# Experts' outputs scattered to their tokens' places by indirect writes, the last block combined by products

## The chip, the cores and the metric

The kernel runs on one core of a Trainium2 chip. Its engines work side by side, each on its own stream of instructions in order: PE (TensorE, matrix products and transposes; PEld is its weight load), DVE (VectorE), ACT (ScalarE), POOL (GpSimd) and SP (SyncE, which here only issues DMAs). SP's and ACT's DMAs go through hardware queues; POOL's, the indirect ones among them, through a software queue whose descriptors POOL builds itself. The metric is the device time of one execution in microseconds (us), the median over runs.

## What is computed

The reference is an attention layer, then a conditioned low-rank layer feeding a transformer block whose feed-forward part is a mixture of experts. Only the last part is touched by the change:

```python
logits = x @ router_weight                       # 8192 tokens, 8 experts
probs = jax.nn.softmax(logits, axis=-1)
top_p, top_i = jax.lax.top_k(probs, 2)
top_p = top_p / jnp.sum(top_p, axis=-1, keepdims=True)
...
cap = int(np.ceil(N * K / E * 1.25))             # an expert's later tokens are dropped
...
fc1 = gelu(einsum('ech,ehf->ecf', xt, moe_w1))   # 256 -> 512
fc2 = einsum('ecf,efh->ech', fc1, moe_w2)        # 512 -> 256
weighted = fc2 * padded_probs[:, None]
moe_out = zeros((N, H)).at[padded_tid].add(weighted)
return h1 + moe_out                              # and the block's input is added
```

So each of 8192 tokens (256 numbers each) gets the sum of at most two expert outputs, weighted by two probabilities, on top of a residual.

## The kernel before

**Stages.** Stage 1 (loop over `s`, 32 sequences of 256 tokens, to about 360 us) computes the attention layer and the low-rank layer. Its instructions are ordered by a planner; SP loads the input of sequence `s + 3` while `s` is computed. The second stage (loop over `i`, 64 tiles of 128 tokens, to about 690 us) computes the transformer block's attention, writes each token's normalised row to `z2_d` and its residual to `res_d` in HBM. From here on the order on every engine is the order in which the program is written. The third stage runs the experts: the tokens are sorted into *slots*, 256 slots make a *block*, and all tokens of a block go to one expert. Three plans exist, for 54, 62 or 74 blocks; the number is computed on the device and a branch takes one. Here 54 blocks run.

**Routing.** `packed`, `early` and `rest` compute, in small pieces laid between blocks, for each token its two slots (`slots`), and by products with one-hot matrices (`p_tab`, L1572) the inverse: for each slot the token's number (`rows_of` writes it to `src_row`). The first 11 blocks come from the first 48 tiles alone (`early`), so that they can start before the last tiles are done. The token's number travels as the upper 16 bits of a float: `rowbits` holds `IDBASE + token`, and `rows_of` shifts it back and subtracts `IDBASE`. `yrow` holds, for each token, its two slots, and `prob` its two weights, set to zero where the token was dropped.

**One block n.** `gather(n)` (L763) is two indirect DMAs on POOL, each fetching 128 rows of 1 KB from `z2_d`; it is issued three blocks ahead and waits for one of four buffers. `turn_in` (L783, L787) transposes the rows on PE and scales them on DVE. `weights` (L775) copies the expert's weights. `hidden` (L797, L801) makes 16 products and the gelu on ACT; `result` (L809) makes 16 products, ACT copies them to `ys` (L813, two buffers), and SP writes the block's 256 rows to `y_d` in slot order (L814).

**Bringing rows back.** 16 groups of four tiles. From block 20 the loop is in `experts`. Group g is fetched when block `ready[g]` has come: at 22, 24, 26 and so on, and the last one after all 54. `fetch_rows` (L1694) issues for each tile two indirect DMAs on POOL that fetch its tokens' expert rows from `y_d[:upto]`, where `upto` is the number of slots that are then written; SP reads the group's residual `rs` (L1688). `combine` (L1705) is two DVE operations a tile: row times weight plus residual. Four DMAs on SP (L1711) write a group's output. In one block's time POOL is given two gathers and four of these fetches. Order on POOL in loop pass n: `gather(n + 3)`, then the fetches of up to two tiles.

**Waits.** The program declares no semaphores: the framework orders an instruction behind earlier ones that touch the same part of a buffer, in SBUF, PSUM or HBM. The views that are passed to indirect DMAs are cut by hand in two places: early gathers name `z2_d[: 3 * PACK * P]`, and the fetches name `y_d[:upto]`.

Of the kernel before, what the change touches and what calls it, by code (L numbers as in the profile page):

```python
# [9 lines left out]
F32 = mybir.dt.float32  # L10
I32 = mybir.dt.int32
BF16 = mybir.dt.bfloat16
AF = mybir.ActivationFunctionType
ALU = mybir.AluOpType
AX = mybir.AxisListType
PSUM = bass.MemoryType.PSUM
DRAM = bass.MemoryType.DRAM

P = 128
S = 32  # L20
T = 256
D = 256
# [3 lines left out]
NTOK = S * T  # L26
NJ = NTOK // P
# [12 lines left out]
EARLY = 3  # L40
IDBASE = 96 * 128
DR = D + NE
# [7 lines left out]
def block_kernel(ctx: ExitStack, tc: tile.TileContext, a: dict, out: bass.AP):  # L50
# [20 lines left out]
    res_d = dram.tile([NSG, P, 4 * D], F32, name="res_d")  # L71
    y_d = dram.tile([NB * BLK, D], F32, name="y_d")
    fac_d = dram.tile([S, RANK, 2 * D + NE], F32, name="fac_d")
# [36 lines left out]
    with ExitStack() as c1:  # L110
# [456 lines left out]
        for b in range(4):  # L567
# [37 lines left out]
        nc.vector.memset(freshc[:, :, 0], 0.0)  # L605
        rowbits = const.tile([P, NJ], I32, name="rowbits")
        nc.gpsimd.iota(rowbits, pattern=[[P, NJ]], base=IDBASE, channel_multiplier=1)
        nc.vector.tensor_scalar(rowbits, rowbits, 16, None, ALU.logical_shift_left)
        rb2 = const.tile([P, NJ, 2], BF16, name="rb2")
        nc.vector.tensor_copy(  # L610
            rb2, rowbits.bitcast(F32).unsqueeze(2).to_broadcast([P, NJ, 2])
        )
# [14 lines left out]
        prow_s = const.tile([P, 1], F32, name="prow_s")  # L627
        nc.vector.tensor_scalar(prow_s, prow, float(BLK), None, ALU.mult)

        wqkv = load(const, "wqkv", [P, 2, 384], a["wqkv"].rearrange("(c p) m -> p c m", p=P))  # L630
# [15 lines left out]

        rb2c = const.tile([P, PACK, 2], BF16, name="rb2c")
        for q in range(3):
            for b in range(4):
                r = SURE * (4 * q + b)  # L650
                nc.sync.dma_start(
                    out=rb2c[r : r + SURE],
                    in_=rb2[32 * b : 32 * b + SURE, PACK * q : PACK * (q + 1)],
                )
# [21 lines left out]
        head.close()  # L676

        for s in range(2, S + 1):  # L680
            if s + 3 < S:
                load_x(s + 3)
            if s < S:
                softmax(s)
# [51 lines left out]
    gap = keep.tile([P, NJ], F32, name="gap")  # L736
    yrow = keep.tile([P, NJ, 2], I32, name="yrow")
    src_row = keep.tile([P, NB, 2], I32, name="src_row")
    eids = [keep.tile([1, P], I32, name=f"eid{i}") for i in range(2)]
    plan = keep.tile([P, 1], I32, name="plan")  # L740
# [3 lines left out]
    bothc = keep.tile([P, 2 + NE * PACK], BF16, name="bothc")  # L744
    slots1 = keep.tile([P, NJ, 2], F32, name="slots1")
    in1 = keep.tile([P, NE, 3 * PACK], BF16, name="in1")
    other = keep.tile([P, NE, 3 * PACK], BF16, name="other")
    nc.gpsimd.memset(slots1, 0.0)
    nc.gpsimd.memset(in1, 0.0)
# [55 lines left out]
    def result(n, ps):  # L805
        we2 = wcs[n % 2][:, 1].rearrange("p (c d) -> p c d", c=4)
        for h in range(2):
            for f in range(4):
                nc.tensor.matmul(  # L809
                    ps[:, h, :], lhsT=hts[n % 2][:, f, h * P : (h + 1) * P],  # L810
                    rhs=we2[:, f, :], start=(f == 0), stop=(f == 3),
                )
        nc.scalar.copy(yss[n % 2], ps)  # L813
        nc.sync.dma_start(  # L814
            out=y_d[BLK * n : BLK * (n + 1), :].rearrange("(p h) d -> p h d", h=2),
            in_=yss[n % 2],
        )

# [18 lines left out]
    with ExitStack() as c2:  # L837
# [276 lines left out]
        def early():  # L1114
# [95 lines left out]
            for q in range(3):  # L1210
                for b in range(4):
                    r, rows = SURE * (4 * q + b), slice(32 * b, 32 * b + SURE)
                    js = slice(PACK * q, PACK * (q + 1))
                    nc.sync.dma_start(
                        out=slots1[rows, js, :].rearrange("p j k -> p (j k)"),
                        in_=slots[r : r + SURE],
                    )
                    nc.sync.dma_start(
                        out=in1[rows, :, js], in_=by_expert(inc)[r : r + SURE]
                    )  # L1220
# [24 lines left out]
            for i in range(n2):  # L1245
# [3 lines left out]
                )  # L1249
            rows_of(ps[:, :nbc], cut(nbc, I32), src_row[:, :EARLYB, :])  # L1250
            begun.append(True)
# [38 lines left out]

        def rows_of(table, tab, rows):


            nc.vector.tensor_scalar(tab, table.bitcast(I32), 16, None, ALU.logical_shift_right)
            nc.vector.tensor_scalar(
                rows.rearrange("p n h -> p (n h)"), tab, IDBASE, 0, ALU.subtract, ALU.max
            )
# [90 lines left out]
    with tc.tile_pool(name="rt", bufs=1) as rt, tc.tile_pool(  # L1388
# [24 lines left out]
        def rest():  # L1413
# [165 lines left out]
            for g in range(0, n2 // 8 + 2, 2):  # L1579
# [3 lines left out]
                for k in range(g, min(g + 2, n2 // 8)):  # L1583
# [8 lines left out]
                    columns(rows, col[:, 16 * k : 16 * k + 16], nbc)  # L1592
                    numbered(rows, rb2[:, 4 * k : 4 * k + 4])
                    ready.append((oh, wid, k))
                    yield 1.8
            rows_of(p_tab, rt.tile([P, nbc], I32, name="tab"), src_row[:, EARLYB:, :])
            begun.append(True)
# [23 lines left out]
            for k in range(2):  # L1621
                nc.vector.tensor_scalar(
                    prob[:, :, k], half, 0.5 - k, 0.5, ALU.mult, ALU.add
                )

            all_ = slots1.rearrange("p j k -> p (j k)")
            moved = rt.tile([P, n2], F32, name="moved")
            nc.vector.tensor_scalar(
                moved, slots, 0.0, float(EARLYB * BLK), ALU.is_gt, ALU.mult
            )  # L1630
            nc.vector.tensor_tensor(moved, moved, slots, ALU.add)
            nc.vector.tensor_tensor(moved, moved, all_, ALU.add)
            yield 1.0
            probf = prob.rearrange("p j k -> p (j k)")
            nc.vector.scalar_tensor_tensor(probf, moved, 0.0, probf, ALU.is_gt, ALU.mult)
            nc.vector.tensor_scalar(
                yrow.rearrange("p j k -> p (j k)"), moved, -1.0, 0.0, ALU.add, ALU.max
            )
            yield 0.4

# [36 lines left out]

    def experts(count, ready, w3):

        groups = [{} for _ in range(NSG)]  # L1680

        def fetch_rows(j):

            g, i = j // 4, j % 4
            v = groups[g]
            if i == 0:
                v["rs"] = w3.tile([P, 4, D], F32, name="rs")
                nc.sync.dma_start(  # L1688
                    out=v["rs"].rearrange("p j d -> p (j d)"), in_=res_d[g]
                )  # L1690
            upto = ready[g] * BLK
            for k in range(2):
                yg = v[i, k] = w3.tile([P, D], F32, name=f"yg{k}", bufs=8)
                nc.gpsimd.indirect_dma_start(  # L1694
                    out=yg, out_offset=None, in_=y_d[:upto, :],
                    in_offset=bass.IndirectOffsetOnAxis(ap=yrow[:, j, k : k + 1], axis=0),
                )

        def combine(j):
            g, i = j // 4, j % 4  # L1700
            v = groups[g]
            if i == 0:
                v["ot"] = w3.tile([P, 4, D], F32, name="ot")
            for k in range(2):
                nc.vector.scalar_tensor_tensor(  # L1705
                    v["ot"][:, i, :], v[i, k], prob[:, j, k : k + 1],
                    v["rs"][:, i, :] if k == 0 else v["ot"][:, i, :], ALU.mult, ALU.add,
                )
            if i == 3:
                for b in range(4):  # L1710
                    nc.sync.dma_start(  # L1711
                        out=out_v[b, :, 4 * g : 4 * g + 4, :],
                        in_=v["ot"][32 * b : 32 * b + 32],
                    )


        fetched, due = 0, []
        for n in range(AHEAD, count):
            if n + 3 < count:
                gather(n + 3)  # L1720
            for f2 in range(2):
                hidden(n, f2, p_hs[f2])
            if n + 1 < count:
                turn_in(n + 1, p_x)
                weights(n + 1)
            result(n, p_ys[n % 2])
            while due and due[0][0] <= n:
                combine(due.pop(0)[1])
            for _ in range(2):
                if fetched < NJ and ready[fetched // 4] <= n:  # L1730
                    fetch_rows(fetched)
                    due.append((n + 2, fetched))
                    fetched += 1
        while due or fetched < NJ:
            while fetched < NJ and len(due) < 8:
                fetch_rows(fetched)
                due.append((0, fetched))
                fetched += 1
            combine(due.pop(0)[1])

    def arm(count, ready):
        with tc.tile_pool(name="w3", bufs=2) as w3, tc.manual_schedule():
            experts(count, ready, w3)

# [62 lines left out]
```

## Time and profile before

| | us |
|---|---|
| median of 15 runs | 1136.94 (1133.82 to 1143.35) |
| the profiled execution | 1138.14 |
| its span | 1136.4 |
| PE busy in it | 1056.5 (93%) |
| POOL busy | 509.5 (45%) |
| DVE busy | 680.0 (60%) |
| ACT busy | 411.9 (36%) |

A profile is one execution, recorded by the hardware. Its span runs from the first to the last recorded work; 1.7 us lie around it. In tables of groups, `L763` is line 763 of the kernel; a line reads *line, engine, operation, output <- inputs, number of instructions | busy us, mean ns of one | idle us of the engine just before them, and what ended most of it*. In the chain of waits and the timeline the first number is the start in us from the span's beginning, the second the length. The slices cut the span into 40 equal parts of 28.4 us; a digit is the busy share in tenths. "To landing" is the time from a DMA's issue until what waits for it can go on.

### The profile page before, as it was taken

What the parts mean: (1) busy time and instruction counts of PE and PEld (TensorE: products, weight loads), DVE (VectorE), ACT (ScalarE), POOL (GpSimd) and SP (SyncE); (2) the same over time, 40 slices, a digit from 0 to 9 for tenths busy, and PEclk for the clock granted to TensorE, in tenths of its full rate; (3) what the DMA queues carried; (4) which work ended last, traced back from release to release, by engine and by line L of the source; (5) the groups of instructions that cost most, each with busy time, mean ns of one, the idle gap of its engine ahead of it and who ended that gap; (6) DMA issues with size and microseconds to landing.
All of it is one profiled execution on the core that took longest, in us unless ns stands there. A gap on an engine that the chain in (4) does not pass through costs nothing.

```text
span 1136.4 us, 16889 instructions
## 1 busy us (share of the span) xinstructions
PE 1056.5 (93%) x5723; PEld 855.4 (75%) x5724; DVE 680.0 (60%) x1676; ACT 411.9 (36%) x953; POOL 509.5 (45%) x687
## 2 busy tenths in 40 slices
PE   8999999999994999999999778999999998999992
PEld 5686888888883777777776566888888887887871
DVE  4454555555552688888888886972222554454542
ACT  2222333333332556666665343432222222222220
POOL 2011111111111466666665465213333777777774
PEclk9999999999997999999999998999999999999996
DMA  9552333333262132534343143112223566555665
GB/s 304 140 149 95 102 112 112 112 112 113 84 161 88 58 128 99 188 132 170 126 140 114 39 136 134 65 48 79 72 72 107 181 193 208 179 184 184 198 180 161
DMA packets 88147, 149.50 MB, mean 132 GB/s; under 512 B 13620, under 2 KB 54100, under 8 KB 87508
## 3 DMA queue, kind: packets, MB, share of 16 engines
q1 hardware_dynamic: 72068, 99.97, 27.3%
q0 software_dynamic: 15936, 48.32, 13.9%
q8 instruction: 47, 0.77, 0.3%
q14 instruction: 48, 0.39, 0.1%
q10 hardware_dynamic: 48, 0.05, 0.0%
HBM read 90.86 MB, written 57.22 MB: 130 GB/s over the span
## 4 chain that ended last, share of the span: by engine, by line
PE 51%; issue 24%; DMA 8%; POOL 8%; DVE 7%; SPq 1%; ACT 1%; POOLq 0%; ACTq 0%; DVEq 0%
PE ps_y L809 11%; PE ps_h L797 10%; PE p_qkv L885 6%; DMA yg<-y_d,yrow 4%; PE p_pr L990 4%; PE p_av L956 4%; PE p_sc L915 3%; PE ps_t L944 3%; DMA xx<-z_d,src_row 3%; POOL xx_d L507 2%; POOL o L503 2%; POOL yg L1694 2%; PE ps_xt L783 2%; PE ps_n L846 1%; PE ps_f L271 1%
## 5 line engine op out<-in xcount | busy, mean ns | idle before, releaser
L809 PE MATMUL ps_y<-xx,ht 128*128 128x256 f32 x864 | 201.5, 387 | 0.0
L797 PE MATMUL ps_h<-xt,xx 128*128 128x256 f32 x864 | 195.8, 379 | 0.0
L809 PEld LDWEIGHTS ps_y<-xx,ht 128*128 128x128 f32 x864 | 164.1, 195 | 21.6 <-ACT ht L801 0.3
L797 PEld LDWEIGHTS ps_h<-xt,xx 128*128 128x128 f32 x864 | 163.6, 190 | 22.1
L763 POOL DMA_INDIRECT xx<-z_d,src_row x108 | 122.3, 1133 | 128.3 <-PE ps_xt L783 76.9
L787 DVE TENSOR_SCALAR xt<-ps_xt,ln 128x256 f32<-128x256 f32 x106 | 52.7, 539 | 194.8 <-PE ps_xt L783 194.8
L1694 POOL DMA_INDIRECT yg<-y_d,yrow x128 | 135.2, 1056 | 55.8 <-issue 28.8
L502 POOL TENSOR_SCALAR ve<-mv 128x2 f32<-128x2 f32 x32 | 6.9, 217 | 255.1 <-DVE mv L103 255.1
L801 ACT ACTIVATE ht<-ps_h 128x512 f32<-128x512 f32 x108 | 64.5, 597 | 127.4 <-PE ps_h L797 127.2
L813 ACT COPY ys<-ps_y 128x512 f32<-128x512 f32 x54 | 31.6, 586 | 189.3 <-PE ps_y L809 174.7
L885 PE MATMUL p_qkv<-wqkv,lnt 128*128 128x384 f32 x256 | 94.4, 492 | 0.0
L935 POOL TENSOR_TENSOR sc<-sc,mx 128x512 f32<-128x512 f32 x64 | 66.9, 1046 | 52.1 <-DVE mx L934 47.9
L895 ACT COPY vbd<-p_qkv 32x64 f32<-32x64 f32 x256 | 52.5, 205 | 94.9 <-DVE qk L891 92.7
L956 PEld LDWEIGHTS p_av<-vbd,pt 128*128 128x128 f32 x512 | 67.0, 192 | 18.9 <-ACT pt L949 3.7
L990 PE MATMUL p_pr<-wp,ao 128*128 128x264 f32 x256 | 71.8, 403 | 3.1 <-DVE h L994 3.0
L995 POOL TENSOR_TENSOR res<-h,xx 128x256 f32<-128x256 f32 x64 | 43.7, 683 | 62.3 <-DVE h L994 60.2
L378 PE MATMUL p_z<-yt,m_qk 128*128 128x256 f32 x256 | 67.2, 389 | 0.8 <-ACT yt L363 0.8
L495 PE MATMUL p<-layer,x1t 128*128 128x264 f32 x256 | 65.9, 401 | 2.1 <-ACT x1t L485 1.5
L956 PE MATMUL p_av<-vbd,pt 128*128 128x68 f32 x512 | 65.1, 270 | 1.5 <-ACT pt L949 1.5
L391 PE MATMUL p_v<-w_vo,yt 128*128 128x256 f32 x256 | 60.6, 379 | 0.0
L495 PEld LDWEIGHTS p<-layer,x1t 128*128 128x128 f32 x256 | 46.8, 193 | 15.6 <-ACT x1t L485 7.4
L885 PEld LDWEIGHTS p_qkv<-wqkv,lnt 128*128 128x128 f32 x256 | 44.4, 193 | 18.3 <-ACT lnt L849 1.1
(312 smaller groups left out, 1844.1 us busy)
## 6 DMA issues: line engine op xcount, KB each, us to landing
xx_d<-o POOLq DMA_DIRECT2D x32, 530.0 KB, 3.4
y_d<-ys SPq DMA_DIRECT2D x54, 256.0 KB
xx<-xx_d SPq DMA_DIRECT2D x13, 1060.0 KB
xt<-in_x_t_dram SPq DMA_DIRECT2D x32, 256.0 KB
xs<-in_x_dram SPq DMA_DIRECT2D x32, 256.0 KB
wall<-in_moe_w_dram SPq DMA_DIRECT2D x16, 512.0 KB
z_d<-h SPq DMA_DIRECT2D x16, 512.0 KB
res_d<-res SPq DMA_DIRECT2D x16, 512.0 KB
```

The costliest lines, as they stand in the source:

```text
L378: nc.tensor.matmul(p_z[:, m, :], lhsT=m_qk[:, c, m * P : (m + 1) * P], rhs=yt[:, c, :], start=(c == 0), stop=(c == 1),)
L391: nc.tensor.matmul(p_v[:, t, :], lhsT=yt[:, c, t * P : (t + 1) * P], rhs=w_vo[:, c, :], start=(c == 0), stop=(c == 1),)
L495: nc.tensor.matmul(p_2, lhsT=v["x1t"][:, c, t * P : (t + 1) * P], rhs=v["layer"][:, c, :], start=(c == 0), stop=(c == 1),)
L763: nc.gpsimd.indirect_dma_start(out=xgs[n % 4][:, h, :], out_offset=None, in_=z2_d[: 3 * PACK * P, :] if n < EARLYB else z2_d[:, :], in_off ...
L797: nc.tensor.matmul(ps[:, i, :], lhsT=we1[:, c, f * P : (f + 1) * P], rhs=xts[n % 2][:, c, :], start=(c == 0), stop=(c == 1),)
L801: nc.scalar.activation(hts[n % 2][:, 2 * f2 : 2 * f2 + 2, :], ps, AF.Gelu_apprx_tanh)
L809: nc.tensor.matmul(ps[:, h, :], lhsT=hts[n % 2][:, f, h * P : (h + 1) * P], rhs=we2[:, f, :], start=(f == 0), stop=(f == 3),)
L885: nc.tensor.matmul(ps, lhsT=live2[n // 4]["lnt"][:, c, j * P : (j + 1) * P], rhs=wqkv[:, c, :], start=(c == 0), stop=(c == 1),)
L935: nc.gpsimd.tensor_tensor(sc, sc, mx.unsqueeze(2).to_broadcast([P, 16, S]), ALU.subtract)
L956: nc.tensor.matmul(p_a[:, g // 2, :, g % 2, :], lhsT=v["pt"][:, g, :], rhs=vbd[n % 5][:, g], start=True, stop=True,)
L990: nc.tensor.matmul(p_p, lhsT=tiles[n]["ao"][:, gp, :], rhs=wp2[:, gp, :], start=(gp == 0), stop=(gp == 1),)
L1694: nc.gpsimd.indirect_dma_start(out=yg, out_offset=None, in_=y_d[:upto, :], in_offset=bass.IndirectOffsetOnAxis(ap=yrow[:, j, k : k + 1], a ...
```

## The change

The expert's rows no longer go to `y_d` in slot order, to be fetched by token; they are written straight to the token's place and read back in plain transfers.

- `y_d` becomes 2 x 8192 rows, one for each token and each of its two choices, and 128 dump rows for empty slots. `rowbits` counts tokens once for each choice, `IDBASE` becomes 8192, and `rows_of` makes two tables: `src_row` (the token) and `dst_row` (the place in `y_d`, or the partition's dump row where the slot is empty).
- `result` issues two indirect writes on POOL, 128 rows of 1 KB each, instead of one plain write on SP.
- Stage 1 fills `y_d` with zeros, in 64 plain writes of 256 KB on SP, three in each pass from `s = 4`, so that rows of dropped tokens read as zero; `yrow` and the zeroing of `prob` go.
- `fetch_rows` reads a group's rows in four plain DMAs of 256 KB on SP, ahead of `hidden(n)` in the order. The loop's order on POOL becomes `gather(n + 3)`, then the scatters of block n.
- In the plans of 54 and 62 blocks the last block is not written to `y_d`. The last group is read one block earlier; what the last block adds to its 512 tokens is computed by products on PE with a matrix `own` that holds each token's weight at its slot. `own` is prepared in blocks 20 to 24: per tile three DVE operations, two transposes and one copy.

```diff
-    y_d = dram.tile([NB * BLK, D], F32, name="y_d")
+    y_d = dram.tile([2 * NTOK + P, D], F32, name="y_d")
...
+            for n in range(3 * s - 12, min(3 * s - 9, NTOK // P)) if s > 3 else ():
+                nc.sync.dma_start(
+                    out=y_d[2 * P * n : 2 * P * (n + 1), :].rearrange("(p r) d -> p (r d)", r=2),
+                    in_=zeros,
+                )
...
         nc.scalar.copy(yss[n % 2], ps)
-        nc.sync.dma_start(
-            out=y_d[BLK * n : BLK * (n + 1), :].rearrange("(p h) d -> p h d", h=2),
-            in_=yss[n % 2],
-        )
+        for h in range(2):
+            nc.gpsimd.indirect_dma_start(
+                out=y_d[:, :], in_=yss[n % 2][:, h, :], in_offset=None,
+                out_offset=bass.IndirectOffsetOnAxis(ap=dst_row[:, n, h : h + 1], axis=0),
+            )
...
-        def rows_of(table, tab, rows):
+        def rows_of(table, tab, more, ns):
             nc.vector.tensor_scalar(tab, table.bitcast(I32), 16, None, ALU.logical_shift_right)
             nc.vector.tensor_scalar(
-                rows.rearrange("p n h -> p (n h)"), tab, IDBASE, 0, ALU.subtract, ALU.max
+                src_row[:, ns, :].rearrange("p n h -> p (n h)"), tab, NTOK - 1, 0,
+                ALU.bitwise_and, ALU.bitwise_or,
+            )
+            nc.vector.tensor_scalar(more, tab, 0.0, dump[:, 0:1], ALU.is_equal, ALU.mult)
+            nc.vector.scalar_tensor_tensor(
+                dst_row[:, ns, :].rearrange("p n h -> p (n h)"), tab, -float(IDBASE), more,
+                ALU.add, ALU.add,
             )
...
+        def mark(i):
+            ms = []
+            for k in range(2):
+                m = w3.tile([P, 2, P], F32, name=f"mark{k}")
+                nc.vector.tensor_scalar(
+                    m, pos, at_row[:, i, k : k + 1], prob[:, end + i, k : k + 1],
+                    ALU.is_equal, ALU.mult,
+                )
+                ms.append(m)
+            nc.vector.tensor_tensor(ms[0], *ms, ALU.add)
+            marks[i] = ms[0]
+
+        def turn_marks(i):
+            ps = w3p.tile([P, 2, P], F32, name="p_mark")
+            for h in range(2):
+                nc.tensor.transpose(ps[:, h, :], marks[i][:, h, :], ident)
+            nc.scalar.copy(own[:, :, i, :], ps)
+
+        def result_alone():
...
+            p_own = w3p.tile([P, 4, D], F32, name="p_own")
+            for i in range(4):
+                for h in range(2):
+                    nc.tensor.matmul(
+                        p_own[:, i, :], lhsT=own[:, h, i, :], rhs=ys[:, h, :],
+                        start=(h == 0), stop=(h == 1),
+                    )
+            return p_own
...
-            upto = ready[g] * BLK
-            for k in range(2):
-                yg = v[i, k] = w3.tile([P, D], F32, name=f"yg{k}", bufs=8)
-                nc.gpsimd.indirect_dma_start(
-                    out=yg, out_offset=None, in_=y_d[:upto, :],
-                    in_offset=bass.IndirectOffsetOnAxis(ap=yrow[:, j, k : k + 1], axis=0),
-                )
+            y = v["y"] = w3.tile([P, 2, 4, D], F32, name="y")
+            src = y_d[: 2 * NTOK].rearrange("(k g i j p) d -> k g i p j d", k=2, g=NSG, i=2, p=P)
+            for i in range(2):
+                for k in range(2):
+                    nc.sync.dma_start(out=y[:, k, 2 * i : 2 * i + 2, :], in_=src[k, g, i])
...
         for n in range(AHEAD, count):
             if n + 3 < count:
                 gather(n + 3)
+            if fetched < NSG and ready[fetched] <= n:
+                fetch_rows(fetched)
+                due += [(n + 1 + i // 2, fetched, i) for i in range(4)]
+                fetched += 1
             for f2 in range(2):
                 hidden(n, f2, p_hs[f2])
...
+        if alone:
+            for i in range(4):
+                ot = groups[NSG - 1]["ot"][:, i, :]
+                nc.vector.tensor_tensor(ot, p_own[:, i, :], ot, ALU.add)
+                if i % 2:
+                    put(NSG - 1, i - 1, i + 1, [nc.sync, nc.scalar])
```

`put` issues a group's output DMAs, four per call; for the last group two calls of half the tiles each, two DMAs on SP's queue and two on ACT's.

## The prediction

> **What bounds the kernel now.** I read the page first (slices, costliest groups, landings), then the chain of waits for the experts, the waits of that stretch, and GpSimd's timeline in it.
>
> ```profile
> PE   8999999999994999999999778999999998999992
> POOL 2011111111111466666665465213333777777774
> ...
> L763 POOL DMA_INDIRECT xx<-z_d,src_row x108 | 122.3, 1133 | 128.3 <-PE ps_xt L783 76.9
> L1694 POOL DMA_INDIRECT yg<-y_d,yrow x128 | 135.2, 1056 | 55.8 <-issue 28.8
> ```
>
> The 108 gathers are 54 blocks of two, so the 54-block plan ran. PE is near full wherever the experts run; the last slice is nearly empty. GpSimd jumps from 3 to 7 tenths about 865 us, where the row fetches (`yg`) begin. GpSimd's timeline shows what 7 tenths means:
>
> ```profile
> 933.03 1.98 POOL L763 DMA_INDIRECT xx<-z_d,src_row  x1 [0.30 <-issue]
> 935.32 1.00 POOL L763 DMA_INDIRECT xx<-z_d,src_row  x1 [0.30 <-issue]
> 936.63 0.95 POOL L1694 DMA_INDIRECT yg<-y_d,yrow  x1 [0.30 <-issue]
> 937.88 0.95 POOL L1694 DMA_INDIRECT yg<-y_d,yrow  x1 [0.30 <-issue]
> 939.13 0.95 POOL L1694 DMA_INDIRECT yg<-y_d,yrow  x1 [0.30 <-issue]
> 940.38 1.42 POOL L1694 DMA_INDIRECT yg<-y_d,yrow  x1 [0.30 <-issue]
> 942.10 0.95 POOL L763 DMA_INDIRECT xx<-z_d,src_row  x1 [0.30 <-issue]
> ```
>
> An indirect DMA costs GpSimd 0.95 + 0.30 = 1.25 us, now and then 2. The six here take 933.03 to 942.10, 9.1 us without a gap: GpSimd is full. PE's pace and its loss are in the chain:
>
> ```profile
> 766.53 3.45 PE ps_h L797 x16
> ...
> 862.02 3.45 PE ps_h L797 x16
> ...
> 1106.68 3.45 PE ps_h L797 x16
> ...
> PEld ps_xt L783 <- DMA xx<-z_d,src_row: 14.7, 9, 3.1
> PE ps_xt L783 <- DMA xx<-z_d,src_row: 11.5, 7, 2.8
> POOL yg L1694 <- DMA y_d<-ys: 11.8, 3, 11.2
> ```
>
> From 766.53 to 862.02 are 13 blocks: 7.345 us each, PE alone. 862.02 starts block 22 (28 blocks of gathers follow it, 26 to 53) and 1106.68 starts block 53: 244.7 us for 31 blocks, where 31 x 7.345 = 227.7. So **17 us** are lost, and the waits on `xx<-z_d` say to what: gathers that leave late. The second loss is the **tail**: PE ends at 1113.8, the span at 1136.4, 22.6 us of y write, eight fetches at 1.25, combines and four output DMAs.
>
> **The change, part by part.**
>
> *Six indirect DMAs a block become four.* 128 fetches go, 106 scatters come. At 1.25 us that is 5.0 a block, under 7.345. If nothing else waited, the 17 us would come back.
>
> *What a scatter waits for.* The trace of before has none, so the wait is read from the program. There a wait follows the view that an instruction names: the code cuts the fetch's source to `y_d[:upto]`, and the first fetch left at 865.47, as soon as block 21's write (issued 862.72) had landed, with block 22's not yet made. Every scatter now names all of `y_d[:, :]`, so I expect each to be ordered behind the one before it, and padding slots do go to the same dump rows. It is also ordered behind the last plain read of y_d, and each read behind all scatters. On GpSimd the second scatter of a block then stands until the first has landed, and the next block's two gathers stand behind it.
>
> The prices. **L**, scatter issue to landing: the nearest row is the gather, same queue and size.
>
> ```profile
> DMA to landing us min/median/max: 2.7/2.8/4.1
> ...
> DMA to landing us min/median/max: 2.7/3.6/5.9
> ...
> xx_d<-o POOLq DMA_DIRECT2D x32, 530.0 KB, 3.4
> ```
>
> The first line is the gather between 760 and 862 us, the second after 1000, with GpSimd full; GpSimd's own writes to HBM (four times the bytes) take 3.4. The lower bound is SP's write of 256 KB, 862.72 to 865.17 = 2.45; the upper 3.7, the fetches' median. I take 3.0: the quiet gather plus a little, since fewer are in flight. The Trainium skill ("DMA: Bandwidth & Descriptors", Anatomy of one DMA) fits a GpSimd DMA as 2.0 us plus bytes over 436 GB/s, an estimate of 2.3 for 128 KB; no row here goes below 2.45, and by 2.3 the sum below would be 34 us lower, 1125.
>
> **F**, one group's read: four SP issues of 256 KB at about 0.45 (out_dram: 4 in 1.77) put the last at 1.35, and it lands some 3 later (the 512 KB `rs` read is 2.96 in the chain): 4.35; all four hold 1 MB, twice `rs`, so I take 4.7, between 4.0 and 5.5.
>
> Count from landing to landing of a block's second scatter, with 0.1 a handoff. A block without a read: GpSimd issues two gathers after it, 1.25 + 2.5 - L = 0.75 us past the landing, then L + 0.1 + L: L + 3.85 = **6.85**. A block with a read: the read starts at the landing, the scatter waits for it: F + 0.1 + 2L + 0.1 = **10.9**. The pair takes 17.75; PE needs 14.69. So this chain, not PE, sets the pace: `ys` has two buffers, a copy waits for the scatter of two blocks before, ACT's gelu waits behind the copy, PE behind that.
>
> The sum, on this execution's own clock. Block 21's copy ends at 862.7; its scatters have landed at 868.85. Reads are due in blocks 22, 24, 26, 28, 30, 32, 34, 37, then every second to 51: 15 of the 31 blocks 22 to 52. 15 x 10.9 + 16 x 6.85 = 273.1, to 1141.95. The last group's read (block 53) adds 4.7: 1146.65.
>
> *The last block by products.* Its y write, eight fetches and their landings go from the tail. Eight transposes of 128 x 128 come on PE (four take 0.44: 0.9 us), eight products of 0.22 (1.8 us), twelve small DVE operations (0.3 to 0.5 each). With the chain above all of this is covered: PE waits longer than that, and the products end before the last read lands. Without the cover the transposes cost 0.9. What stays behind the last read: eight combines of 0.49 = 3.9, four adds of about 0.55 = 2.2, then the outputs. Before, the last combine ended at 1129.99 and the span 6.4 later with four issues on SP; two on each of two queues save 0.9: 5.5. Together 11.6: span **1158.3**, which is +21.9.
>
> *Zeros.* 64 writes of 256 KB on SP in stage 1. From 100 to 360 us the DMA share is 0.35 at 111 GB/s; 16.8 MB more makes about 0.55. SP's issues (64 x 0.4 us) are spread over 22 sequences. I put it at 0: the loads stand three sequences (28 us) ahead, and that hides a landing that is a few us later. Bounds 0 to +3.
>
> *Small edits.* `rows_of` has two more DVE operations after the one that the gathers wait for; `at_row` replaces five operations near the end of `rest`; twelve SP DMAs of `slots1` go; the tables are twice as wide in elements that are broadcast anyway. All lie beside PE work: gather 11 left at 760.5 for a transpose at 777.3, so 12 us would have to go first. 0, bounds -1 to +1. In blocks 0 to 21 no reads are due, 6.85 is under 7.345 and the gather still leaves more than 5 us before its transpose: 0.
>
> Sum: 1136.94 (median; this execution took 1138.14, its span is 1136.4) + 21.9 = **1159**. L counts 48 times (30 in the blocks with a read, 16 in the others, 2 at the start), F 16 times: 0.1 us of L is 4.8 us, 0.1 of F is 1.6.
>
> The Trainium skill (same page, Two DMAs through the same engine are not ordered) says that one queue doesn't order two writes and that the issuing engine has to wait for the first one's completion. It speaks against this change: GpSimd would pay that wait 31 times; without it the sum is the first rival's.
>
> **Rivals.**
>
> *A. The two scatters are not held apart.* For it: the 1.25 us rhythm of the fetches, none of which waits for another. Against: fetches only read. Then PE sets the pace: block 53 starts at 862.02 + 227.7 + 0.9 = 1090.6, block 52's copy ends about 1091.3, its scatters have landed at 1095.6 (1.25 + 3.0), read 4.7, and 11.6: 1111.9, that is -24.5: **1112**. A read then delays a scatter by some 2 us, which the next block takes back.
>
> *B. The waits are there, but short.* With L at 2.6 and F at 4.5 the sum falls by 48 x 0.4 + 16 x 0.2 = 22.4: **1136**, no change. At F 4.7 the sign turns at L = 3.0 - 21.9 / 48 = 2.54; with both at their lower bounds (2.45, 4.0) the sum is 1121, faster. For it: SP's write of 2.45, and that a write needs no data back. Against: the gather never went under 2.7.
>
> *C. The waits are long.* Scatters go to 128 scattered rows beside reads and gathers: L 3.5, F 5.0 give 24 + 4.8 more: **1188**. For it: 3.6 in the loaded stretch. Against: that stretch had GpSimd's queue full.
>
> *D. The loss isn't GpSimd's.* Then the relief brings nothing and, without ordering waits, only the tail falls, -7.5: **1129**. Against: the waits name `xx<-z_d`.
>
> **How the numbers follow.** The forecast (waits bind, L 2.7 to 3.3) 0.55, C 0.17, B 0.10, A 0.16, D 0.02. The likeliest's own range is 1140 to 1180. Both signs hold weight, so the range reaches from A to C: 1111 to 1188. Slower by over 0.2% (2.3 us, about what this kernel's measurement can tell from none): forecast and C, 0.72. B is split in faster 0.06, same 0.03 and slower 0.01; with A and D faster is 0.24, same 0.03, slower 0.73.
>
> **What would show it.** Right: on GpSimd from 865 us the second scatter of a block starts about L after the first, not 1.25; scatters wait for `y<-y_d` every second block; ACT's copy or PE waits for GpSimd's scatters; blocks take about 8.9 us on the mean. Wrong: two scatters 1.25 apart with PE gapless at 7.345 (A), or L near 2.5 (B). Also wrong if stage 1, up to 360 us, grows by more than 3 us, or if the tail past the last read isn't near 11.6.

## The result and the profile after

The changed kernel takes **1220.57 us** (median of 9 runs, 1217.93 to 1225.85) beside 1137.49 for the kernel before (47 runs): ratio 1.0727, interval 1.0711 to 1.0743. It is slower by 83 us, where +22 was forecast, and above the upper end of the range, 1188. The profiled execution has a span of 1214.2, 77.8 more than the 1136.4 before; it is the shortest of the changed kernel's executions, whose spans run to 1224.1. Beside two series of the experiments below the kernel before was listed with 1199 to 1222 us at a granted clock of 0.95; in three others it read 1138 to 1139, the reason isn't known, and no ratio is taken from those two.

The first view is the page of the changed kernel: slices, then two of its costliest groups.

```profile
PE   8999999999959999999978799999988788787871
...
POOL 2021211111113666666645654566554444435420
...
L827 POOL DMA_INDIRECT y_d<-ys,dst_row x106 | 120.6, 1137 | 229.2 <-DMA y_d<-ys,dst_row 99.5
...
L825 ACT COPY ys<-ps_y 128x512 f32<-128x512 f32 x53 | 31.1, 586 | 243.2 <-DMA y_d<-ys,dst_row 125.8
```

A slice is 30.4 us here (28.4 before). Up to the 29th, which ends at 880 us, PE's row tells the same as before. The 16.8 MB of zeros in stage 1 cost nothing that can be seen: `hidden` of block 22 starts at 862.42 us (862.02 before), while over the profiles of all versions that start varies by 6 us. From the 30th slice on PE falls from 9 to 7 and 8 tenths; the first read was issued at 870.91. GpSimd, mostly 7 tenths before, is mostly at 4: it has less to do and stands. The last column says at what: 99.5 us for scatters already sent. ACT's copy waits 125.8 us for the scatter that frees `ys`. The waits from 860 to 1215 us (total, times, longest):

```profile
ACT ys L825 <- DMA y_d<-ys,dst_row: 125.8, 16, 11.1
...
POOL y_d L827 <- DMA y<-y_d: 78.5, 12, 8.8
...
POOL y_d L827 <- DMA y_d<-ys,dst_row: 63.4, 34, 3.3
...
PE ps_h L809 <- DVE xx L787: 36.6, 13, 5.2
```

Scatters wait for reads 78.5 us in 12 waits and for one another 63.4 us in 34. Three more of the fifteen waits behind a read (21.7 us) stand in this view under `out_dram`, the outputs issued right behind the read. PE's 36.6 us are waits for the copy of the weights on DVE, which stands in order behind combines that wait for the read and what was issued behind it. One pair of blocks on GpSimd (start, length, operation, idle before it and what ended that):

```profile
930.32 1.94 POOL L775 DMA_INDIRECT xx<-z_d,src_row  x1 [0.30 <-issue]
932.57 0.96 POOL L775 DMA_INDIRECT xx<-z_d,src_row  x1 [0.30 <-PE ps_y L821]
939.30 1.00 POOL L827 DMA_INDIRECT y_d<-ys,dst_row  x1 [5.77 <-DMA y<-y_d]
942.01 0.99 POOL L827 DMA_INDIRECT y_d<-ys,dst_row  x1 [1.71 <-DMA y_d<-ys,dst_row]
943.30 1.58 POOL L775 DMA_INDIRECT xx<-z_d,src_row  x1 [0.31 <-issue]
945.18 0.98 POOL L775 DMA_INDIRECT xx<-z_d,src_row  x1 [0.30 <-issue]
946.47 1.00 POOL L827 DMA_INDIRECT y_d<-ys,dst_row  x1 [0.30 <-issue]
949.18 1.68 POOL L827 DMA_INDIRECT y_d<-ys,dst_row  x1 [1.71 <-DMA y_d<-ys,dst_row]
```

and SP's queue beside it:

```profile
931.47 1.93 SPq L1751 DMA_DIRECT2D y<-y_d  x4
933.44 0.47 SPq L1753 DMA_DIRECT2D rs<-res_d  x1
934.01 2.59 SPq L1767 DMA_DIRECT2D out_dram<-ot  x4
952.31 2.63 SPq L1751 DMA_DIRECT2D y<-y_d  x4
```

From the read's first issue to the scatter it holds back are 939.30 - 931.47 = **7.83 us** (mean of fifteen: 8.08), the *hold* of a read. The chain of waits divides it (start, length, what):

```profile
931.47 0.38 SPq L1751
...
932.93 5.50 DMA y<-y_d
...
939.30 1.00 POOL y_d L827
```

The last of the four issues starts 1.46 us after the first, its DMA takes 5.50 us to land, and 0.87 pass until the scatter. The second scatter of a block leaves 2.71 us after the first. From read to read are 20.84 us for two blocks; PE needs 14.69. In this pair GpSimd stands for no more than 0.3 us behind PE and never behind ACT: its chain sets the pace, and PE's wait for DVE lies beside it. The windows show the DMA engines meanwhile (stretch, its length, busy and count of PE, PEld, DVE, ACT, POOL; then granted clock, DMA share, GB/s):

```profile
932.00:933.00 1.00, 1.00 (x7) 0.87 (x6) 0.00 (x0) 0.23 (x1) 0.69 (x2) 1.00 0.38 86
933.00:934.00 1.00, 1.00 (x6) 0.90 (x5) 0.00 (x0) 0.35 (x1) 0.53 (x1) 1.00 1.02 286
934.00:935.00 1.00, 1.00 (x6) 0.87 (x6) 0.00 (x0) 0.49 (x1) 0.00 (x0) 1.00 0.99 331
935.00:936.00 1.00, 1.00 (x7) 0.80 (x5) 0.00 (x0) 0.11 (x1) 0.00 (x0) 1.00 1.02 329
936.00:937.00 1.00, 0.25 (x2) 0.00 (x0) 0.00 (x0) 0.60 (x1) 0.00 (x0) 1.00 1.29 263
937.00:938.00 1.00, 0.00 (x0) 0.00 (x0) 0.00 (x0) 0.00 (x0) 0.00 (x0) 1.00 0.70 151
```

From 933 to 937 the engines are full (share about 1). The read's own 1.05 MB and the 0.26 MB of two gathers would be some 4 us at these rates; whose bytes moved when, the windows don't say, and `rs` and outputs were sent from 933.44 on. At 936.25 PE runs dry. The granted clock, 0.959 on the mean of the execution against 0.976 before, is 1.00 from 931 to 953, so it is not what makes this pair long.

### The profile page after: what moved, and what is told of

It reads as the page before. It is cut to its first block, busy times and chain, and to the rows that moved or that the text cites. A ratio compares the mean times of both kernels' runs of the same rounds, so it can differ in the third digit from the quotient of the medians.

```text
span 1214.2 us, 16927 instructions
## 1 busy us (share of the span) xinstructions
PE 1084.2 (89%) x5747; PEld 870.3 (72%) x5748; DVE 685.7 (56%) x1693; ACT 413.8 (34%) x958; POOL 495.1 (41%) x666
## 4 chain that ended last, share of the span: by engine, by line
PE 40%; issue 26%; DMA 13%; POOL 9%; DVE 6%; SPq 3%; ACT 1%; ACTq 0%; POOLq 0%; DVEq 0%
PE ps_h L809 7%; PE ps_y L821 6%; PE p_qkv L898 6%; DMA y_d<-ys,dst_row 6%; DMA y<-y_d 5%; PE p_pr L1003 4%; PE p_av L969 4%; PE p_sc L928 3%; POOL y_d L827 3%; PE ps_t L957 3%; POOL xx L775 2%; POOL xx_d L509 2%; SPq L1751 2%; POOL o L505 2%; DMA out_dram<-ot 1%
## 5 line engine op out<-in xcount | busy, mean ns | idle before, releaser
L809 PE MATMUL ps_h<-xt,xx 128*128 128x256 f32 x864 | 214.1, 404 | 36.6 <-DVE xx L787 36.6
L809 PEld LDWEIGHTS ps_h<-xt,xx 128*128 128x128 f32 x864 | 174.5, 204 | 68.2 <-DVE xx L787 42.0
L827 POOL DMA_INDIRECT y_d<-ys,dst_row x106 | 120.6, 1137 | 229.2 <-DMA y_d<-ys,dst_row 99.5
L821 PE MATMUL ps_y<-xx,ht 128*128 128x256 f32 x848 | 195.4, 384 | 0.0
L821 PEld LDWEIGHTS ps_y<-xx,ht 128*128 128x128 f32 x848 | 159.7, 193 | 20.3
L825 ACT COPY ys<-ps_y 128x512 f32<-128x512 f32 x53 | 31.1, 586 | 243.2 <-DMA y_d<-ys,dst_row 125.8
L1760 DVE SCALAR_TENSOR_TENSOR ot<-y,prob,rs 128x256 f32<-128x256 f32 x64 | 30.7, 480 | 144.8 <-DMA out_dram<-ot 114.7
```

The source lines that it names most:

```text
L809: nc.tensor.matmul(ps[:, i, :], lhsT=we1[:, c, f * P : (f + 1) * P], rhs=xts[n % 2][:, c, :], start=(c == 0), stop=(c == 1),)
L821: nc.tensor.matmul(ps[:, h, :], lhsT=hts[n % 2][:, f, h * P : (h + 1) * P], rhs=we2[:, f, :], start=(f == 0), stop=(f == 3),)
L827: nc.gpsimd.indirect_dma_start(out=y_d[:, :], in_=yss[n % 2][:, h, :], in_offset=None, out_offset=bass.IndirectOffsetOnAxis(ap=dst_row[:, ...
```

## The experiments

Two theories. **Mine:** the loss is the two ordering waits, scatter behind read and scatter behind scatter, and the miss lies in how long a read takes. **Rivals:** only one of the waits counts; the read isn't slow but disturbed by what stands beside it; or the products of the last block cost the time. Spans are of the profiled execution: 1136.4 before, 1214.2 after. Most versions ran once; since spans of the unedited changed kernel run from 1214.2 to 1224.1, a difference of a few us between two of them says nothing.

### Reads and zeros get a tensor of their own (x_reads_apart)

```diff
+    r_d = dram.tile([2 * NTOK, D], F32, name="r_d")
...
-            src = y_d[: 2 * NTOK].rearrange("(k g i j p) d -> k g i p j d", k=2, g=NSG, i=2, p=P)
+            src = r_d.rearrange("(k g i j p) d -> k g i p j d", k=2, g=NSG, i=2, p=P)
```

> The groups' plain reads (and the zeros of stage 1) use a tensor of their own that no scatter writes; the scatters are unchanged, still ordered behind one another. It leaves out the experts' contribution, except the last block's, so the output is not the reference's; the traffic is the same. Theory (the chain read - two scatters one after the other - read sets the pace): with the reads out of the chain GpSimd needs 2.7 + 1.3 + 2.9 = 6.9 us a block, under PE's 7.345, so blocks come at 7.35 us and the span is 1108 to 1118, some 100 us under the changed kernel. Rival (the scatters and plain reads are more than the DMA engines can carry, or DVE's combines block PE): the span stays above 1170. Rival (the scatter-after-scatter wait alone does it): above 1180.

Measured: span 1155.8, 58 less, but not the expected 1108 to 1118. No scatter waits for a read any more; scatters still wait for one another, and longer (total, times, longest):

```profile
POOL y_d L828 <- DMA y_d<-ys,dst_row: 92.9, 34, 7.0
```

In the changed kernel these were 63.4 us, at most 3.3. The read's bytes now flow while scatters do; what that does to a scatter is shown below. Taking away one wait fed the other.

### The second scatter goes to a second tensor (x_halves_apart)

```diff
-                out=y_d[:, :], in_=yss[n % 2][:, h, :], in_offset=None,
+                out=(y_d, y2_d)[h][:, :], in_=yss[n % 2][:, h, :], in_offset=None,
```

> The second scatter of each block goes to a second tensor that is never read, so that it is no longer ordered behind the first nor behind the reads; half of the experts' rows are left out of the sum, so the output is not the reference's. Theory: a block with a read costs 8.2 (read) + 2.5 (landing) = 10.7 us, one without 5.5; the pair 16.2 against PE's 14.7, so the chain still leads by a little: span 1120 to 1145. Rival (the wait between the halves does nothing, the read alone is the matter): stays above 1180.

Measured: span 1139.2, as expected, with reads as slow as ever (7.95 us). Here a read also no longer waits for a block's second scatter. With -58 above and -75 here the parts add to more than the 77.8 lost, so they can't be added up: what one edit takes away the other takes away in part too.

### A quieter read (x_quiet_reads)

The load of `rs` stands ahead of the read, and all combines of a group come one block after it, so that outputs have left before the next read.

> Each group's residual is read before its rows, not behind them, and all four tiles are combined one block after the read, so that the output writes leave before the next read and not right behind it; all else as in the changed kernel. Theory (a read takes about 8 us in place of 4.7 because 0.5 MB of residual and 0.5 MB of output, issued behind it on SP, share the 16 DMA engines): the read falls to 5 to 5.5 us from its first issue to the scatter it holds back, 16 times 3 us less: span 1160 to 1172. Rival (the rows are slow to read, 1 KB each, whatever else moves): the read stays at 7 to 8 us and the span above 1195.

Measured: span 1208.9, as the rival had it. The read's hold fell to 6.70 us, between the theory's 5 to 5.5 and the rival's 7 to 8: 1.38 us go with `rs` and the outputs, most of its length is its own. The span gained less than fifteen times that: the outputs now move while scatters do. One second scatter with its landing, 4.29 us, ACT's copy that waits for it, and the next scatter, in the chain of waits:

```profile
943.00 4.29 DMA y_d<-ys,dst_row
...
947.39 0.60 ACT ys L825
...
948.06 1.00 POOL y_d L827
```

Scatters wait 22.0 us in 13 waits for ACT's copies, which they don't do in the changed kernel.

### The last block back to scatters, no products (x_no_products)

> The last block goes back to scatters and its group is read after them, as all others; the products, marks and transposes are gone. Theory: one more pair of scatters (about 7 us) stands before the last read, and products, adds and the split of the outputs go (about 1 us): span 1218 to 1226, so the products are worth 4 to 12 us and are not what made the kernel slower. Rival (the products and their preparation cost time): the span falls below 1214.

Measured: span 1217.1, just under the expected range. The last read is issued 6.9 us later (1199.01 for 1192.15), as the theory said, but the span is only 2.9 us longer, less than the spread of the changed kernel. What the products are worth is not shown beyond that; they are not where the loss is.

### Scatters name only groups not yet read (x_views_cut)

Groups lie in falling order behind the dump rows, and block n's scatters name only the rows up to those of groups still open. A scatter then doesn't touch what a read has been sent for.

```diff
-                out=y_d[:, :], in_=yss[n % 2][:, h, :], in_offset=None,
+                out=y_d[: P + 8 * P * open_, :], in_=yss[n % 2][:, h, :], in_offset=None,
...
-                result(n, p_ys[n % 2])
+                result(n, p_ys[n % 2], sum(r > n for r in ready))
```

> y_d is laid out with the groups in falling order behind the dump rows, and a scatter of block n names only the rows up to the groups that are not yet complete; so no scatter is ordered behind a read of a finished group any more. Reads still wait for the scatters before them, scatters for one another. Theory: the read leaves the chain, what is left is the scatter behind the scatter, and its landing is longer while a read is on its way (4 to 6 us in place of 2.7, as in the run with reads in a tensor of their own): span 1150 to 1170. Rival (the read's wait for the scatters sets the pace too): above 1190. Rival (only the wait for reads matters): PE's pace, below 1122.

Measured: span 1181.8, 32 less, though above the expected 1150 to 1170. No scatter waits for a read. GpSimd's timeline, with a read issued at 927.20:

```profile
928.62 1.75 POOL L828 DMA_INDIRECT y_d<-ys,dst_row  x1 [0.30 <-issue]
936.48 0.99 POOL L828 DMA_INDIRECT y_d<-ys,dst_row  x1 [6.12 <-DMA y_d<-ys,dst_row]
```

The scatter now leaves 1.4 us after the read's first issue and doesn't wait for it, but the next one stands 7.86 us: a scatter among a read's bytes lands late. Landings of scatters from 1000 to 1085 us, in the changed kernel and in this one:

```profile
DMA to landing us min/median/max: 2.4/2.4/3.6
```

```profile
DMA to landing us min/median/max: 2.4/2.5/7.7
```

### Rows of their own for empty slots, scatters independent (x_free_rows)

Every slot now has a row of its own in `y_d` (empty ones in 74 x 256 dump rows, enough for the longest plan), so scatters may be declared independent of one another; a memset of one element stands behind each. Scatter behind read stays.

```diff
+DUMPS = 2 * NB * P
...
+            tc.declare_no_dep(scatter.ins, group="scatter", query=mybir.DependencyQuery.ANY_SYNC, reason="each slot has a row of its own")
+            tc.add_to_no_dep_group("scatter", scatter.ins)
```

> Every block and half has 128 dump rows of its own, so that no two scatters write one row, and the scatters are declared independent of one another (a one-element memset stands between them on GpSimd); reads and scatters still wait for each other. Theory: a pair of blocks costs two scatters, two gathers and two scatters at 1.3 each on GpSimd, 2.5 to land and 8 for the read: about 17.5 us against 20.8: span 1150 to 1172. Rival (scatter behind scatter is the whole loss): PE's pace, below 1122. Rival (it costs nothing): 1205 and more.

Measured: span 1167.8, as expected. The hold of a read is the same (8.10 us), but the two scatters after it now leave 1.31 us apart:

```profile
932.28 1.00 POOL L832 DMA_INDIRECT y_d<-ys,dst_row  x1 [6.37 <-DMA y<-y_d]
933.29 0.09 POOL L838 MEMSET gap__3191<- 1x1 f32 x1
933.59 0.99 POOL L832 DMA_INDIRECT y_d<-ys,dst_row  x1 [0.21 <-issue]
```

### Both edits (x_free_cut, free_cut_again)

> Both edits together: views cut and scatters independent. What is left is a read's wait for the scatters before it, which nothing waits for but the combine a block later. Theory: GpSimd needs 4 x 1.3 us and now and then 1 more, under PE's 7.345, so PE sets the pace: block 53 starts at 1091, the last scatters land at 1096.5, the read takes 8, combines and adds 5.2, the outputs 7.6: span 1117, 1110 to 1124, and under the kernel before the change by 1 to 2.3%. Rival (the DMA engines or DVE can't keep up with reads, residual and outputs): above 1136.

> The version with rows of their own for empty slots, scatters independent, and scatters naming only groups not yet read: 1119 to 1123 us, as on the other chip, ratio to the kernel before 0.981 to 0.986.

Measured: 1120.75 us (6 runs), ratio to the kernel before 0.9833 (0.9807 to 0.986); in a second series 1123.45 (4 runs), 0.9853 (0.9816 to 0.9889), its median 0.45 us above the expected range. With both waits gone the change is faster than the kernel before, by 1.5 to 1.7%, clear of the interval. Neither edit alone is (spans 1181.8 and 1167.8 against 1136.4).

### Half the read (x_half_read)

```diff
-                for k in range(2):
+                for k in range(1):
                     nc.sync.dma_start(out=y[:, k, 2 * i : 2 * i + 2, :], in_=src[k, g, i])
...
-                    v["ot"][:, i, :], v["y"][:, k, i, :], prob[:, 4 * g + i, k : k + 1],
+                    v["ot"][:, i, :], v["y"][:, 0, i, :], prob[:, 4 * g + i, k : k + 1],
```

> Reads only the first-choice rows of a group (0.52 MB in place of 1.05 MB, two DMAs in place of four); the second choice is left out of the result. If the time from a read's first issue to the scatter it holds back (8.08 us on average in the changed kernel) is set by bytes at some 350 GB/s: 0.52 MB less is 1.5 us less, so 6.6 us, and over fifteen held blocks plus the last read a span near 1214.2 - 16 x 1.5 = 1190 (1184 to 1196). Rival, that it is a fixed delay of a read from memory after a write, whatever its size: 7.6 us or more and a span above 1206.

Measured: span 1192.9, as the theory of bytes expected, but in another way. The hold fell by 3.05 us to 5.03, twice what was expected, and the second scatter behind it was then late. Half the read is also half the issues: two take 0.90 us where four took 1.93, so by estimate 1.0 of the 3.05 is SP's issuing and 2.0 goes with the bytes. SP's queue, then GpSimd's:

```profile
933.37 0.90 SPq L1751 DMA_DIRECT2D y<-y_d  x2
934.30 0.47 SPq L1753 DMA_DIRECT2D rs<-res_d  x1
934.88 1.98 SPq L1767 DMA_DIRECT2D out_dram<-ot  x4
```

```profile
937.77 1.00 POOL L827 DMA_INDIRECT y_d<-ys,dst_row  x1 [3.30 <-ACT ht L813]
942.59 1.70 POOL L827 DMA_INDIRECT y_d<-ys,dst_row  x1 [3.83 <-DMA y_d<-ys,dst_row]
```

The second scatter stands 4.82 us behind the first (4.13 on the mean, 2.78 in the changed kernel): `rs` and the outputs are still moving. Over a pair of blocks (mean from read to read) 0.52 MB and two issues less gave 21.43 - 20.15 = 1.28 us. A read's length isn't a fixed delay.

### The load of rs in the block between (x_rs_between)

```diff
...
+            elif 0 < fetched < NSG and "rs" not in groups[fetched]:
+                fetch_rs(fetched)
```

> The 0.52 MB load of rs moves from behind the read of its group to the block between two reads; the combines stay where they are. If rs shares the DMA engines with the read in front of it, the read holds its scatter for up to 1.5 us less (6.6 to 7.3 us in place of 8.08): span 1192 to 1204. Rival, that rs is served behind the read and never slowed it: about 8 us and a span of 1210 to 1218, or more, since the scatters of the block between then share the engines with rs.

Measured: span 1205.9, hold 7.87 us. The hold is the rival's: `rs` behind the read on SP's queue hardly slows it (0.2 us). The span lies between the two expected ranges. With the 1.38 us of the quieter read, about 1.2 would then be the outputs'; they weren't moved alone.

### Both edits and rs in the block between (x_free_cut_rs, free_cut_rs_again)

> The version without waits between scatters and finished reads (1120.8 us median, span 1117.7), with rs moved to the block between two reads. There nothing waits for a read but its combine, so only the last read gains, where rs no longer stands behind it: 9.2 us from its issue to the first combine becomes 7 to 8, span 1115.5 to 1117.5, a ratio to the kernel before of 0.981 to 0.984. Rival, that rs is served behind the read and costs it nothing: no change, 1117 to 1119.

> The same with the load of rs moved to the block between two reads: 1115 to 1118 us, 3 to 5 us below the version that loads rs behind its read, because the last read then has nothing behind it. Rival, that the 1116 us seen was the other chip's: within 1 us of that version.

Measured: 1116.34 us (6 runs), and in the second series, beside 1123.45 for the version with `rs` behind the read, **1116.75** (4 runs), ratio to the kernel before **0.9803** (0.9776 to 0.983). The 6.7 us between the medians are more than the expected 3 to 5, but the four runs of that version spread over as much (1118.77 to 1125.53). In its GpSimd timeline a scatter follows another without waiting for its landing:

```profile
925.78 1.00 POOL L833 DMA_INDIRECT y_d<-ys,dst_row  x1 [2.03 <-ACT ys L831]
...
927.09 0.99 POOL L833 DMA_INDIRECT y_d<-ys,dst_row  x1 [0.21 <-issue]
...
928.38 0.99 POOL L781 DMA_INDIRECT xx<-z_d,src_row  x1 [0.22 <-PE ps_h L815]
929.67 1.38 POOL L781 DMA_INDIRECT xx<-z_d,src_row  x1 [0.31 <-issue]
933.13 1.00 POOL L833 DMA_INDIRECT y_d<-ys,dst_row  x1 [2.08 <-ACT ys L831]
```

and PE starts a block every 7.345 us, its own pace:

```profile
924.68 3.62 PE L815 MATMUL ps_h<-xt,xx 128*128 128x256 f32 x16
...
932.02 3.62 PE L815 MATMUL ps_h<-xt,xx 128*128 128x256 f32 x16
...
939.37 3.62 PE L815 MATMUL ps_h<-xt,xx 128*128 128x256 f32 x16
```

The gain over the other version is in the tail. DVE's first and last combine of the last group:

```profile
1101.47 0.48 DVE L1778 SCALAR_TENSOR_TENSOR ot<-y,prob,rs 128x256 f32<-128x256 f32 x1 [5.30 <-DMA y<-y_d]
...
1106.86 0.48 DVE L1778 SCALAR_TENSOR_TENSOR ot<-y,prob,ot 128x256 f32<-128x256 f32 x1
```

The read is issued at 1098.47, so the first combine starts 3.0 us after it (expected were 7 to 8) and the last ends 8.9 after it, combines running while the rest lands. In the other version the first, for which `rs` behind the read must have come too, starts 9.2 us after its read (1101.18 to 1110.39), and the last ends 13.0 after it. These 4.1 us are the gain that `rs` explains. The other version's read was also issued 2.7 us later; that isn't the work of `rs`, for in that version's other profile it was issued at 1096.26.

### Both kernels unedited, again

> The kernel before the change, unedited, on the same chip as the three others, so that they can be put against it: span 1133 to 1140, time 1134 to 1143 us.

> The kernel before, unedited. Theory: 1134 to 1144 us at a granted clock near 0.975, span near 1135, whatever the chip. Rival, that it has a second speed on some chips: 1199 to 1222 us at a clock near 0.95.

> The changed kernel, unedited. Theory: 1216 to 1226 us, so some 80 us over the kernel before on the same chip. Rival: no difference to the kernel before on a chip where that reads 1199 to 1222 us.

> The kernel before, unedited. Theory: span 1134 to 1142 us at a granted clock near 0.975. Rival, a second speed: a span of 1197 to 1220 at a clock near 0.95; then the profile has the lost time in the experts' stage, as waits of PE for gathers, or spread over all stages, as a lower clock.

> The changed kernel, unedited, on the same chip: span 1212 to 1222 us at a clock near 0.958, as twice before; and 77 us above the kernel before, or, where that has its second speed, within 1 per cent of it.

Measured: before 1138.01 (12 runs), 1139.07 (10 runs) and 1138.65 (one); after 1219.13 (4 runs), ratio 1.071 (1.0678 to 1.0742), and 1223.42 (one). The difference stands, and the rivals of a second speed were not met.

## Why the prediction was right or wrong

**Right: what binds.** The views decide the waits, scatter behind scatter and scatter behind read, and GpSimd's chain with them sets the pace, with ACT's copy and PE behind it. Each wait was removed alone and both together, and only with both gone do the 17 us that gathers lost come back (PE gapless at 7.345).

**Wrong: the step "F, one group's read", 4.7 us, bounds 4.0 to 5.5.** It measured 8.08 on the mean, 7.1 at the least, its handoff included (4.8 in the sum). The step priced the read as the start of the last issue, 1.35, plus the 2.96 us landing of `rs`, which is half the bytes, and allowed 0.35 for the other half. In the pair shown the last issue started at 1.46, so that wasn't the miss; its DMA landed 5.50 later where 3.35 were put, and the handoff was 0.87, put at 0.1. The landing of `rs` can't stand for a read of 1.05 MB that with two gathers fills all sixteen DMA engines. Of the 3.28 us missing, 1.38 went when `rs` and outputs were moved out of the way; the other 1.90 stayed with the read and the gathers. The half read shows that bytes are part of it, by the estimate above 2.0 us for 0.52 MB; how much is left that neither bytes nor issues explain stays open.

**Wrong size: L, 3.0.** From the first scatter to the second are 2.71 us in most blocks, 2.83 on the mean, where the sum had 3.1 with its handoff. The landing is 2.4; the row nearest in kind (the gather, 2.8) was farther off than SP's write of 2.45. Rival B was nearer in this half, but not in F.

**Wrong size: GpSimd's issues.** Three between scatters were put at 1.25 each, 3.75; from 942.01 to 946.47 the trace has 4.46, one of the gathers taking 1.58; the mean of sixteen is 4.55.

In the pair shown: F 7.83 for 4.8, twice 2.71 for 3.1, 4.46 for 3.75, 3.13 from the last scatter to the read for 3.0: 20.84 for 17.75.

**The sum.** The span missed by 1214.2 - 1158.3 = 55.9 us: block 21's scatters landed at 870.91 for 868.85 (+2.06); the 31 blocks took 321.24 for 273.1 (+48.1: F 15 x 3.28 = 49.2; scatter to scatter 87.7 for 96.1, -8.4; last scatter to read 39.5 for 45, -5.5; issues 72.8 for 60, +12.8); from the last read to the first combine passed 9.3 for 4.7 (+4.6); combines 3.75 for 3.9 and adds 1.35 for 2.2 (-1.0); outputs 7.65 for 5.5 (+2.15). So F is 49.2 of it. The 4.6 at the last read aren't F alone: its combine also waits for `rs` behind it, which the sum put at nothing, and with `rs` moved the tail was 4.1 us shorter.

**Rivals.** A (1112) fell in this kernel; the version with both edits and `rs` between came near it, 1116.75. C had the sign and the place but put the length into L. D fell: with the waits gone, relief of GpSimd gains.

**Costed at nothing.** The zeros and the small edits were put at 0: block 22 starts 0.4 us later, less than it varies from profile to profile. The transposes and products were said to be covered: without them the span is 2.9 longer, within the spread.

## What to carry to other kernels

Before rows are written by indirect DMA, list what each write's view touches: in this kernel every later write and read within that view was ordered behind it, and the issuing engine paid a landing for each. Give writes that can't meet rows of their own, say so, and cut the views so that what has been read is not named; one of the two alone left this kernel slower than before. Price a read by its own bytes and issues beside what moves with it, not by the landing of a smaller one.

## What the runs showed of the hardware

A scatter of 128 rows of 1 KB to HBM landed sooner than the gather of the same size. In the changed kernel from 760 to 862 us, where there are no reads of `y_d` yet, first the scatter, then the gather:

```profile
DMA to landing us min/median/max: 2.4/2.4/4.4
```

```profile
DMA to landing us min/median/max: 2.6/2.8/4.8
```

Among the bytes of a 1 MB read the same scatter took up to 7.7 us. And bytes moved away from one wait came back in the next: half the read shortened the hold by 3.05 us and the pair by 1.28.
